# A one-core hybrid block: prefix sums in two halves with the keys' sums beside them, one more unit's convolution on TensorE, and a new planned order

## The chip, the cores and the metric

The kernel runs on one core of one Trainium2 chip. A time is the device time of one execution in microseconds (us). The time before is the median of three runs, 792.27 us (791.22 to 794.27). Engines are named as in the profile: PE is TensorE (PEld its weight loads), DVE is VectorE, ACT is ScalarE, POOL is GpSimd, SP is SyncE, which issues the transfers.

## The reference, cut to what matters

The input x is 8 sequences of 512 tokens with 128 features, all in float32. Four layers follow each other, each as `x = x + layer(layernorm(x))`:

1. Delta rule (attention a): q, k and v are projections followed by a causal convolution over four tokens and SiLU, 16 heads of 8; a state of 8 by 8 per head is updated token by token.
2. Mixture of experts ("f" in the kernel): 8 experts, the best two per token weighed by a softmax; `relu(x W1) W2` with 256 hidden features.
3. Linear attention (attention b): with phi = elu + 1, token i of a head of width 8 gets

```python
A = jnp.einsum('bhid,bhjd->bhij', q, k) * mask
num = jnp.einsum('bhij,bhjd->bhid', A, v) + jnp.einsum('bhid,bhde->bhie', q, S)
den = jnp.sum(A, axis=-1) + jnp.einsum('bhid,bhd->bhi', q, z) + EPS
out = num / den[..., None]
```

4. The same mixture of experts again ("g").

## The kernel before, in words

The 512 tokens are cut into eight units of 64 tokens (c = 0 to 7). A unit holds the 64 tokens of all eight sequences: four tiles of 128 rows (two sequences of 64 tokens each). Every unit goes through the delta rule, then f, linear attention b and g. The delta rule's recurrence (`recurring`) runs over the units one after another, 16 steps of four DVE instructions each per unit, and ties a later unit to an earlier one, as the convolution's border of three tokens and attention b's carried state do. So layers of early units run beside the recurrence of later ones. Unit 7 is split into two halves after the delta rule (`HALVED`).

**Order.** Every piece of work is a generator that yields the engine that it needs next. A `Weaver` runs them against its own table of durations (`duration`, and `weaver.took(...)` for corrections), with priorities per stream (`FAVOURED`, `OFFSETS`; a thousand tuned numbers), and so writes one fixed order of instructions for each engine. On the chip each engine goes through its list in this order and waits on semaphores. Where the plan has PE idle for at least 0.6 us, `keep_busy` emits filler matmuls ("busy", bf16, 512 columns) for seven tenths of the gap (`BUSY`), so that PE's clock is kept up; the number of fillers in a stretch of PE's list tells how much idle time the plan had there.

**Convolution.** `convolved(s)` handles q, k or v of a unit. For units below `TAPS_ON_PE` (0 to 3) the four taps are four accumulating matmuls of 512 columns with weights `wc` (taps times projection, made at the start by `weights_of_taps`). For the other units one matmul projects, ACT copies the result and scales one tap, POOL moves the 3-token border twice, and DVE adds three taps (`scalar_tensor_tensor` on `s_pp_a`). `wc` lies in the buffers of experts 5 to 7 (`resident[5..7]`), so `loading_later_weights` waits for unit 3's projections before it loads these experts.

**Experts.** `moe` normalizes, computes logits, marks the best two experts on DVE (`first_of_largest`), then weighs them (`relative`: a difference, a tanh, two products) and gets `cb`, a weight per token and expert. `all_experts` transposes `cb` on PE (tile `s_pw`), stores it to DRAM, and for each expert loads the row broadcast over 128 partitions (`wt_xsT<-scw`), multiplies it with the transposed tokens on POOL, and runs two first matmuls (`s_ph`) and two second ones (`y_py`), with a ReLU on ACT between (`hT<-s_ph`).

**Linear attention.** `attend` handles one pair of tiles, 16 times in all. The keys' and values' outer products kv (16 heads x 9 x 8 columns, the ninth column a one, which carries the keys' own sums for the denominator) are made on POOL. `by_q` then takes heads 0 to 5, 6 to 10 and 11 to 15 in turn: four matmuls with a 64 x 64 triangle of ones give the prefix sums over 64 tokens (`s_pc<-kv,tri`, 432 or 360 columns, each in a quarter of PE's array), two DVE products with the queries (`qs`) and one DVE reduce (`nd`) follow. The tile kv has one buffer.

Of the kernel before, what the change touches and what calls it, by code (L numbers as in the profile page):

```python
# [10 lines left out]
F32 = mybir.dt.float32  # L11
# [26 lines left out]
TURNED = 1  # L38
# [3 lines left out]
TAPS_ON_PE = 4  # L42
# [4 lines left out]
ADDED_ON_DVE = (4,5,6,7)  # L47
NEAR_NORMS = (5,6,7)
# [5 lines left out]
TURNED_IN = (0,7)  # L54
# [13 lines left out]
PASSES = ()  # L68

FAVOURED = {  # L70
    ("b", 0.0): 1475, ("b", 1.0): -605, ("b", 2.0): 408, ("b", 3.0): -1141, ("b", 4.0): 1159, ("b", 5.0):
    -397, ("b", 6.0): -3095, ("b", 7.0): -2237, ("b", 7.5): -2071, ("beside",): 1509, ("ending",): 696,
    ("f", 0): 1839, ("f", 1): 922, ("f", 2): 673, ("f", 3): -941, ("f", 4): 1648, ("f", 5): 1050, ("f", 6):
    -1587, ("f", 7): 767, ("f", 7.5): -2892, ("g", 0.0): 1576, ("g", 1.0): 901, ("g", 2.0): 357, ("g", 3.0):
    7212, ("g", 4.0): -253, ("g", 5.0): -2424, ("g", 6.0): -246, ("g", 7.0): 1986, ("g", 7.5): -2626,
    ("outputs",): 7, ("prepare", 0): -904, ("prepare", 1): -3306, ("prepare", 2): 224, ("prepare", 3):
    -1571, ("prepare", 4): -839, ("prepare", 5): -16, ("prepare", 6): 680, ("prepare", 7): -2427, ("recur",
    0): 3219, ("recur", 1): -6342, ("recur", 2): -2844, ("recur", 3): 482, ("recur", 4): -2744, ("recur",
    5): -1405, ("recur", 6): 1064, ("recur", 7): -724, ("values",): 149, None: -1498,
# [4 lines left out]
    -5735, -5206, -179, -62, -5753, 0, -6219, -6323, 29, -6838, 1464, 2372, 2338, -2, 1277, -3446, -3136,  # L84
    2417, -3137, -2112, -3119, -3650, -311, 76, 1, 3, -3, 77, -342, -7970, 977, -20, -4091, 3665, -19, 806,
    -4343, -4621, -4648, -4379, 711, 806, -5289, 1734, 1900, 1275, 623, -5269, -420, -380, -832, -1479, 50,
    -758, -790, 125, -3620, 585, -553, 237, 2322, 2064, -5521, 501, -5381, -5928, -3498, -40, 2563, 4086,
    10628, -5495, 782, 11097, 2142, 524, -2998, -175, 1440, -9862, 334, 747, 94, -5047, -6796, 307, 308,
    -1787, -402, -3506, -63, -187, 265, -2927, -6059, -6411, -6618, 0, -4528, -6371, -6553, -6091, -5056,
    263, -538, -1107, -6503, -6983, -6, -6510, -36, -961, -967, 294, 389, -6742, -8230, -142, -7747, -8737,  # L90
    -7250, -7254, -7665, -422, 1935, 282, -996, -6683, -9031, 177, 1221, 466, 360, -7342, 552, -8817, -42,
    -7371, 101, 1699, 247, 245, 186, -7410, 57, 713, -5151, 127, -91, -80, -5933, 56, -6006, -6402, 412,
    -6116, -445, 35, 2434, -4925, -4928, -4874, -938, 1079, 406, -7960, 775, 519, -186, -183, -6551, -7752,
    -7695, -8113, 429, 2079, 1870, 73, 72, 717, 130, -428, -37, 347, 2267, 385, -69, 3340, -640, -367, 165,
    -831, -1483, 0, 486, -5539, -200, -199, -399, -34, 2547, -7582, -106, -2671, 11037, 1388, 1383, 1120,
    -962, 17, -1270, -6162, -175, -5673, 211, 50, -7246, -2444, -7484, -2599, -386, 24, -1456, -1295, -1542,
    449, 95, 3319, -2490, -5181, -17, 250, 1245, 968, 926, -3459, -1, -51, -7241, -6288, -40, -5786, 456, 0,
    2, -7292, 471, -361, -79, -6239, 1121, 209, 228, 171, -490, -335, -1339, -4313, -4533, -173, -162,
    -1885, -4676, -5235, -6460, -342, -6601, -6575, 266, 235, 4646, 4647, 78, -899, -7489, 388, -348, 4,
    2051, 1488, -3366, -170, -1594, -5834, -4738, -590, -6081, 2703, 771, 806, 2101, -1052, -4471, -334,  # L100
    10046, 384, -6869, -6546, 10224, -8058, 323, -1252, 463, 8950, 0, -8361, 1480, -113, -361, -8416, -9767,
    -47, -200, -9523, 27, -8517, -60, 66, -8349, -229, -9575, -9613, 177, 0, -516, 2087, 1808, 1102, -3472,
    -3462, -3444, -261, -48, -604, -199, 8924, -1499, -2626, 0, -5333, -68, 0, -3882, -1964, 1388, 1387,
    -3692, -5022, -5065, -555, 136, 6558, 1420, 1897, 1801, 9994, 299, 277, 324, -41, 8082, 391, 7156, 7157,
    -5841, -322, -1273, -5351, 627, 9366, -2233, -2747, 1391, 674, -7825, -11438, -30, 775, 2023, 1821,
    -1660, -376, -7698, 679, -3112, 1424, -5849, 0, -55, 151, -899, 680, -7529, -8147, 148, 896, 1077, 914,
    339, 108, 425, -1456, -5019, -1472, -477, 2580, -4207, -3854, -4163, -8696, -1145, -4645, -48, -435,
# [360 lines left out]
def duration(key, op, args, kw):  # L468
# [12 lines left out]
    if key == "ACT":  # L481
        table = TABLE_OF.get(args[2]) if op == "activation" else None
        scale = args[2] if op == "mul" else kw.get("scale", 1.0)
        more = (0.19 if "bias" in kw else 0.0) + (0.0 if isinstance(scale, float) else 0.08)
        return key, 0.2 + more + n * 0.76e-3, 0.1, table
    if key == "POOL" and ALU.pow in args:
        return key, 1.05, 0.1
# [1521 lines left out]
```

## Time and profile before

The numbers below are of one profiled execution. The medians in the first row are of other runs.

| quantity | before |
|---|---|
| median of 3 runs | 792.27 us |
| the profiled execution | 790.81 us, of which the span on the core is 789.1 us |
| PE busy (matmuls) | 758.7 us, 96% of the span |
| DVE / ACT / POOL busy | 560.8 / 504.7 / 446.0 us (71 / 64 / 57%) |
| filler matmuls | 195, busy 52.7 us |
| expert matmuls (`s_ph`, `y_py`, f and g) | 530.7 us busy in all |
| granted PE clock, mean | 0.991 |

By stretches of the span, PE idle (the stretch less PE's busy time) and fillers in it:

| stretch, us | PE idle, us | fillers |
|---|---|---|
| 0 to 40 | 5.8 | 61 |
| 40 to 80 | 4.5 | 34 |
| 80 to 120 | 3.5 | 47 |
| 120 to 160 | 1.4 | 10 |
| 160 to 200 | 7.1 | 28 |
| 200 to 240 | 1.7 | 1 |
| 240 to 760 | 1.6 | 4 |
| 760 to 789 | 4.7 | 10 |

A matmul in float32 is two records in this trace, and a record's modelled end overlaps the next one's start. So the time that a matmul takes from the others is read as the distance from its start to the next start, not as its duration. A busy share is an average: PE is the busiest engine, but in the first 240 us it also waits.

### The profile page before, as it was taken

How to read it: one execution, taken by the hardware profiler on the slowest of the kernel's cores; microseconds unless marked ns; L12 is line 12 of the kernel's file. 1: busy time of each engine (PE TensorE's matmuls, PEld its weight loads, DVE VectorE, ACT ScalarE, POOL GpSimd, SP SyncE). 2: the span in 40 equal slices, each digit the busy share in tenths (PEclk: the TensorE clock that was granted, in tenths of full speed). 3: DMA queues.
4: the chain of work that ended last, by engine and by line, in shares of the span. 5: the costliest groups of instructions: out<-in, count | busy, mean ns of one | idle time of the engine just before them, and what ended most of it. 6: DMA issues, size and time to landing. Idle time of an engine off the chain costs nothing.

```text
span 789.1 us, 11578 instructions
## 1 busy us (share of the span) xinstructions
PE 758.7 (96%) x3383; PEld 384.7 (49%) x3383; DVE 560.8 (71%) x1429; ACT 504.7 (64%) x1388; POOL 446.0 (57%) x609
## 2 busy tenths in 40 slices
PE   8888899997999999999999999999999999999997
PEld 4344454553435434544444435453444456644475
DVE  1689898978997698899999799798557145342310
ACT  5765767688877865678676875773664445643352
POOL 1244447659586495775586664877736606735331
PEclk9999899998999999999999999999999999999999
DMA  1451426105233311214132132232112211321121
GB/s 46 118 133 42 123 63 183 45 23 148 69 97 80 98 56 55 81 55 126 54 111 96 34 102 78 82 106 67 42 41 81 60 28 48 108 69 44 37 60 34
DMA packets 82392, 59.67 MB, mean 76 GB/s; under 512 B 48152, under 2 KB 64152, under 8 KB 82328
## 3 DMA queue, kind: packets, MB, share of 16 engines
q1 hardware_dynamic: 81608, 58.64, 25.8%
q8 instruction: 27, 0.44, 0.2%
q10 hardware_dynamic: 720, 0.28, 0.2%
q14 instruction: 37, 0.30, 0.1%
HBM read 46.52 MB, written 12.39 MB: 75 GB/s over the span
## 4 chain that ended last, share of the span: by engine, by line
PE 78%; DVE 11%; ACT 6%; issue 2%; DMA 2%; POOL 1%; SPq 0%; DVEq 0%; ACTq 0%; POOLq 0%
PE s_ph_f L454 14%; PE y_py_f L454 13%; PE s_ph_g L454 13%; PE y_py_g L454 12%; PE s_pc_b L454 5%; PE s_pp_a L454 4%; PE s_pp_b L454 2%; PE busy L1950 2%; PE s_pu_b L454 2%; DVE st L454 2%; PE s_pS_b L454 2%; DVE W L454 1%; ACT squares L454 1%; DVE pj L454 1%; DVE terms L454 1%
## 5 line engine op out<-in xcount | busy, mean ns | idle before, releaser
L454 ACT ACTIVATE hT_g<-s_ph_g 128x512 f32<-128x512 f32 (+1 forms) x144 | 79.0, 552 | 95.5 <-PE s_ph_g L454 94.5
L454 PE MATMUL y_py_f<-hT_f,resident 128*128 128x512 f32 (+1 forms) x288 | 134.3, 555 | 0.3 <-ACT hT_f L454 0.2
L454 PE MATMUL s_ph_f<-wt_xsT_f,resident 128*128 128x512 f32 (+1 forms) x288 | 132.1, 554 | 1.9 <-POOL wt_xsT_f L454 1.1
L454 PE MATMUL y_py_g<-hT_g,resident 128*128 128x512 f32 (+1 forms) x288 | 133.3, 553 | 0.3
L454 PE MATMUL s_ph_g<-wt_xsT_g,resident 128*128 128x512 f32 (+1 forms) x288 | 131.0, 553 | 0.3 <-POOL wt_xsT_g L454 0.2
L454 ACT ACTIVATE hT_f<-s_ph_f 128x512 f32<-128x512 f32 (+1 forms) x144 | 78.7, 550 | 50.9 <-PE s_ph_f L454 49.4
L454 POOL TENSOR_TENSOR wt_xsT_g<-wt_xsT_g,xn_xnT_g 128x512 f32<-128x512 f32 (+1 forms) x69 | 79.0, 1166 | 37.0 <-DMA wt_xsT_g<-scw_g 26.7
L454 POOL TENSOR_TENSOR po<-st,kq 128x256 f32<-128x256 f32 x128 | 93.8, 763 | 3.3 <-DVE st L454 2.7
L454 POOL TENSOR_TENSOR kv_b<-ph_b,v 128x1152 f32<-128x1152 f32 x32 | 69.2, 2176 | 39.8 <-ACT v L454 27.1
L454 POOL TENSOR_TENSOR wt_xsT_f<-wt_xsT_f,xn_xnT_f 128x512 f32<-128x512 f32 (+1 forms) x69 | 79.4, 1168 | 17.5 <-DMA wt_xsT_f<-scw_f 17.4
L454 DVE TENSOR_TENSOR qs_b<-s_pc_b,ph_b 128x360 f32<-128x360 f32 (+1 forms) x96 | 50.4, 551 | 46.2 <-PE s_pc_b L454 45.5
L454 PEld LDWEIGHTS y_py_f<-hT_f,resident 128*128 128x128 f32 x288 | 50.6, 190 | 47.2 <-issue 40.4
L454 PEld LDWEIGHTS s_ph_f<-wt_xsT_f,resident 128*128 128x128 f32 x288 | 50.4, 190 | 47.4 <-issue 31.6
L454 PEld LDWEIGHTS y_py_g<-hT_g,resident 128*128 128x128 f32 x288 | 50.9, 190 | 44.1 <-issue 35.6
L454 PEld LDWEIGHTS s_ph_g<-wt_xsT_g,resident 128*128 128x128 f32 x288 | 50.9, 190 | 43.7 <-issue 32.0
L454 DVE TENSOR_REDUCE st<-terms 128x64 f32<-128x320 f32 x128 | 61.4, 480 | 12.3 <-ACT terms L454 6.0
L454 DVE TENSOR_REDUCE factors<-pj 128x32 f32<-128x288 f32 x128 | 58.4, 456 | 6.2 <-ACT factors L454 2.5
L1950 PE MATMUL busy<-ones 128*128 128x512 bf16 x195 | 52.7, 411 | 9.5 <-ACT o L454 3.4
L454 DVE TENSOR_TENSOR pj<-st,factors 128x256 f32<-128x256 f32 x128 | 53.4, 417 | 4.7 <-ACT factors L454 1.8
L454 DVE TENSOR_TENSOR terms<-factors,kt 128x256 f32<-128x256 f32 x128 | 53.7, 419 | 4.2 <-ACT vn L454 1.1
L454 ACT COPY terms<-st 128x64 f32<-128x64 f32 x128 | 39.6, 309 | 25.0 <-DVE st L454 23.8
L454 POOL TENSOR_TENSOR pq<-y_a,y_a 128x128 f32<-128x128 f32 x32 | 21.1, 685 | 46.2 <-ACT squares L454 23.1
(270 smaller groups left out, 1336.1 us busy)
## 6 DMA issues: line engine op xcount, KB each, us to landing
wt_xsT_f<-scw_f SPq DMA_DIRECT2D x55, 256.0 KB
wt_xsT_g<-scw_g SPq DMA_DIRECT2D x55, 256.0 KB
scr<-y_a SPq DMA_DIRECT2D x24, 256.0 KB
qk<-scr SPq DMA_DIRECT2D x16, 256.0 KB
x_a<-in_x_dram SPq DMA_DIRECT2D x16, 128.0 KB
vv<-scr SPq DMA_DIRECT2D x8, 256.0 KB
sco<-on SPq DMA_DIRECT2D x8, 256.0 KB
oT<-sco SPq DMA_DIRECT2D x8, 256.0 KB
```

The lines of the kernel that those rows point to most:

```text
L454: r = call(*args, **kw)
L1950: nc.tensor.matmul(pt, ones, ones.unsqueeze(1).to_broadcast([P, 4, P]), start=True, stop=True)
```

## The change

The edits, in the order of the diff:

- `TAPS_ON_PE` goes from 4 to 5: unit 4's taps are matmuls too. PE's list gets 12 matmuls of 512 columns with tap weights and loses 3 plain projections; DVE loses 9 `scalar_tensor_tensor`, ACT 3 copies and 3 scalings, POOL 6 border copies. The border that unit 5 needs is now made in unit 5.
- The tap weights lie in the tile kv instead of in experts 5 to 7. Experts 5 to 7 load at once; the first pair's `attend` waits for unit 4's projections before it takes kv.
- kv has eight columns per head instead of nine. `by_q` takes two halves of eight heads: four matmuls of 512 columns, plus two of 128 columns (`s_pk<-keys,tri`) that sum the keys themselves; a new piece `denominators` multiplies these by the queries in PSUM and reduces them. It takes three PSUM banks at once instead of two.
- The weights of the two best experts (`relative`) start as soon as the second maximum is known, beside the marking of the second expert.
- `cb` lies in a 128 x 128 tile that is zero outside the used columns, and the whole tile is transposed.
- The planner's durations for some ACT and POOL operations are changed, a few fixed corrections are added or removed, the plan gets six more passes (`PASSES`), and all priorities (`FAVOURED`, `OFFSETS`) are new. So the order on every engine is new.

Counted in the two programs, PE's list has 1948 matmuls before and 1943 after, of which 195 and 181 are fillers; DVE's list has 1431 and 1438 instructions, ACT's 1263 and 1257, POOL's 614 and 611, SP's 379 and 379. The options `STATES_ON_PE` and `KEYS_ON_POOL` are empty, and `TURNED` names the same four cases as before.

The diff, cut to its core (the tables of priorities and the code of the empty options are left out):

```diff
-TURNED = 1
+TURNED = {"f0": 1, "g0": 1, "f7": 1, "g7": 1}
 QUERIES_ON_POOL = ()
 ELU_ON_POOL = ()
 CORRECTED_ON_POOL = tuple(range(8))
-TAPS_ON_PE = 4
+TAPS_ON_PE = 5
...
+STATES_ON_PE = ()
+KEYS_ON_POOL = ()
+BURST = NE - 3
...
-TURNED_IN = (0,7)
...
-PASSES = ()
+PASSES = ((1, 0.0, {}), (5, 0.1, {}))
...
-        more = (0.19 if "bias" in kw else 0.0) + (0.0 if isinstance(scale, float) else 0.08)
+        more = (0.1 if "bias" in kw else 0.0) + (0.0 if isinstance(scale, float) else 0.06)
         return key, 0.2 + more + n * 0.76e-3, 0.1, table
     if key == "POOL" and ALU.pow in args:
-        return key, 1.05, 0.1
+        return key, 0.4 + n * 0.16, 0.1
     if key == "POOL":
-        return key, 0.2 + n * (1.72e-3 if n > 512 else 2.0e-3), 0.1
+        if op == "tensor_copy":
+            return key, 0.16 + n * 1.3e-3, 0.1
+        return key, 0.18 + n * (1.73e-3 if n > 512 else 2.15e-3), 0.1
...
-    wc = [resident[NE - 3 + s].rearrange("p (k d) -> p k d", k=4) for s in range(3)]
+    kv_ = const.tile([P, 2, NH, HD, HD], F32, name="kv")
+    taps = kv_.rearrange("p w h e d -> p (w h e d)")[:, 0 : 12 * D].rearrange("p (s k d) -> p s k d", s=3, k=4)
+    wc = [taps[:, s] for s in range(3)]
...
+    cbs = [const.tile([P, P], F32, name=f"cb_{i}") for i in range(SETS)]
+    for i in range(SETS):
+        nc.gpsimd.memset(cbs[i], 0.0)
...
-    kvs = held_in(1, [P, 2, NH, V1, HD], "kv")
-    qss = held_in(1, [P, 2, 6 * V1 * HD], "qs")
+    kvs = Slots(weaver, None, None, "kv", 1, [kv_])
+    qss = held_in(1, [P, 2, NH // 2 * HD * HD], "qs")
...
-            if TAPS_ON_PE and e >= NE - 3:
-                yield fired("projected", TAPS_ON_PE - 1, e - (NE - 3))
             for to, by in [(slice(0, NF), f_w1[e])] + [
                 (slice(NF + f * D, NF + (f + 1) * D), f_w2[e, f * P : (f + 1) * P, :]) for f in range(2)
             ]:
                 yield "SP"
                 sp.dma_start(resident[e][:, to], by)
+                if e >= BURST and to.stop < 2 * NF:
+                    weaver.moves(-LANDS)
...
-            pe.transpose(pt[0 : nb * NE, 0:P], cb.rearrange("p b e -> p (b e)"), ident)
+            pe.transpose(pt[:, 0:P], cb_, ident)
...
-            if e < TURNED and int(name[1]) in TURNED_IN:
+            if e < TURNED.get(name[:2], 0):
...
-        m2 = yield from first_of_largest(lg2, 1)
...
+            if k:
+                scales["weights"] = spawn(relative(m1, m))
...
+        yield from first_of_largest(lg2, 1)
+        yield scales["weights"]
+        cb_ = cbs[own]
+        cb = cb_[:, 0 : nb * NE].rearrange("p (b e) -> p b e", b=nb)
...
+        if c == 0:
+            yield from all_of([fired("projected", TAPS_ON_PE - 1, s) for s in range(3)])
         kv = yield from kvs.take(n)
...
-                .to_broadcast([P, NH, V1, HD]),
-                v1[:, w].unsqueeze(3).to_broadcast([P, NH, V1, HD]),
+                .to_broadcast([P, NH, HD, HD]),
+                v1[:, w, :, 0:HD].unsqueeze(3).to_broadcast([P, NH, HD, HD]),
...
-        def by_q(lo, hi):
-            nh = hi - lo
-            m = nh * V1 * HD
-            yield from banks.need(2)
+        def prefixes(to, i, w, src):
+            of = slice(i * CH, (i + 1) * CH)
+            pe.matmul(to[w * CH : (w + 1) * CH], tri[of, of], src[of, w], start=True, stop=True)
+            if i or w:
+                weaver.overlaps(max(1.68e-3 * free_size(to), 0.225) - 0.01)
+
+        def by_q(half):
+            nh = NH // 2
+            lo, m = half * nh, nh * HD * HD
+            yield from banks.need(3)
             pcs = []
             for i in range(2):
-                pc = yield from banks.take(f"pc_{n}_{lo}_{i}")
+                pc = yield from banks.take(f"pc_{n}_{half}_{i}")
                 pcs.append(pc)
+            pk = yield from banks.take(f"pk_{n}_{half}")
             yield "PE"
             for i in range(2):
-                of = slice(i * CH, (i + 1) * CH)
                 for w in range(2):
-                    pe.matmul(
-                        pcs[i][w * CH : (w + 1) * CH, 0:m], tri[of, of],
-                        kvf[of, w, lo * V1 * HD : hi * V1 * HD], start=True, stop=True,
-                    )
-                    if i or w:
-                        weaver.overlaps(1.68e-3 * m - 0.01)
-            qs = yield from qss.take(f"{n}_{lo}")
+                    prefixes(pcs[i], i, w, kvf[:, :, half * m : (half + 1) * m])
+            for w in range(2):
+                prefixes(pk[:, 0:D], half, w, keys)
+            summing = spawn(denominators(half, pk))
+            qs = yield from qss.take(f"{n}_{half}")
             for i in range(2):
                 yield "DVE"
                 dve.tensor_tensor(
-                    qs[:, i, 0:m].rearrange("p (h e d) -> p h e d", h=nh, e=V1),
-                    pcs[i][:, 0:m].rearrange("p (h e d) -> p h e d", h=nh, e=V1),
-                    queries[:, i, lo * HD : hi * HD].rearrange("p (h d) -> p h d", d=HD).unsqueeze(2)
-                    .to_broadcast([P, nh, V1, HD]),
+                    qs[:, i].rearrange("p (h e d) -> p h e d", h=nh, e=HD),
+                    pcs[i].rearrange("p (h e d) -> p h e d", h=nh, e=HD),
+                    queries[:, i, lo * HD : (lo + nh) * HD].rearrange("p (h d) -> p h d", d=HD).unsqueeze(2)
+                    .to_broadcast([P, nh, HD, HD]),
                     ALU.mult,
                 )
                 banks.give(pcs[i])
@@ -1733,10 +1804,18 @@
                     weaver.moves(-DEPENDENT)
             yield "DVE"
             dve.tensor_reduce(
-                nd[:, :, lo:hi].rearrange("p i h e -> p i (h e)"),
-                qs[:, :, 0:m].rearrange("p i (m d) -> p i m d", d=HD), AX.X, ALU.add,
+                nd[:, :, lo : lo + nh, 0:HD], qs.rearrange("p i (h e d) -> p i h e d", h=nh, e=HD), AX.X, ALU.add
             )
             qss.give(qs)
+            yield summing
+
+        def denominators(i, pk):
+            sums = pk[:, 0:D]
+            yield "DVE"
+            dve.tensor_tensor(sums, sums, queries[:, i], ALU.mult)
+            yield "DVE"
+            dve.tensor_reduce(nd[:, i, :, HD], sums.rearrange("p (h d) -> p h d", d=HD), AX.X, ALU.add)
+            banks.give(pk)
 
...
-        summed = [spawn(by_q(lo, hi)) for lo, hi in ((0, 6), (6, 11), (11, 16))]
+        summed = [spawn(by_q(half)) for half in range(2)]
...
-            weaver.took("POOL", 0.8)
```

## The prediction

> **What bounds the kernel now.** I read the page first: the span, the busy shares and the chain that ended last.
>
> ```profile
> span 789.1 us, 11578 instructions
> PE 758.7 (96%) x3383; PEld 384.7 (49%) x3383; DVE 560.8 (71%) x1429; ACT 504.7 (64%) x1388; POOL 446.0 (57%) x609
> PE   8888899997999999999999999999999999999997
> PE 78%; DVE 11%; ACT 6%; issue 2%; DMA 2%; POOL 1%; SPq 0%; DVEq 0%; ACTq 0%; POOLq 0%
> ```
>
> PE is the bound, and its row of tenths says where it isn't: only in the first third and the last slice does a digit fall below 9. Next I read the busy time by stretches of 40 us (the first number after the stretch's length is PE's).
>
> ```profile
> 160.00:200.00 40.00, 32.89 (x185) 18.26 (x184) 31.88 (x78) 34.25 (x100) 29.84 (x47) 0.91 0.32 92
> 240.00:280.00 40.00, 39.69 (x152) 19.89 (x151) 28.55 (x71) 32.10 (x80) 21.76 (x28) 1.00 0.37 99
> 560.00:600.00 40.00, 40.00 (x192) 18.30 (x190) 21.93 (x52) 23.74 (x58) 20.48 (x18) 1.00 0.27 80
> 760.00:789.00 29.00, 24.32 (x110) 18.18 (x108) 1.12 (x4) 9.99 (x27) 7.54 (x11) 0.99 0.18 42
> ```
>
> From 240 to 760 us PE never rests, while DVE falls from 38 us of 40 to 14. So in this part a microsecond of PE work is a microsecond of span, and relief for DVE, ACT or POOL is worth nothing. Before 240 us PE idles 24.0 us and runs 181 of the 195 fillers; there the recurrence and the first units' chains, not PE, set the pace. The span is thus PE's real work, plus fillers, plus idle, and I cost the change in these three terms.
>
> To price PE's work I read its timeline inside the dense part, taking distances from start to start (columns: start, duration, what).
>
> ```profile
> 311.03 1.12 PE L454 MATMUL y_py_g<-hT_g,resident 128*128 128x512 f32 x2
> 312.09 1.44 PE L454 MATMUL s_pc_b<-kv_b,tri 64*64 64x360 f32 x16
> 313.46 1.13 PE L454 MATMUL y_py_g<-hT_g,resident 128*128 128x512 f32 x2
> 314.42 0.38 PE L454 MATMUL s_pt_q_b<-ident,ph_b 128*128 128x128 f32 x2
> 314.73 0.95 PE L454 MATMUL s_pc_b<-kv_b,tri 64*64 64x432 f32 x8
> 315.62 0.66 PE L454 MATMUL s_pty_g<-ident,m_yT_g 128*128 128x128 f32 x4
> 321.38 0.71 PE L454 MATMUL s_pS_b<-sbd,qT_b 128*64 128x144 f32 x8
> 322.02 1.13 PE L454 MATMUL y_py_f<-hT_f,resident 128*128 128x512 f32 x2
> 326.00 1.02 PE L454 MATMUL s_ph_f<-wt_xsT_f,resident 128*128 128x512 f32 x2
> 326.86 1.02 PE L454 MATMUL y_py_f<-hT_f,resident 128*128 128x512 f32 x2
> ```
>
> A 512-column matmul takes 0.86 us (326.00 to 326.86). Two 360-column groups of four take 1.37 and one of 432 takes 0.89. With a fixed part s and k per column, s + 720 k = 1.37 and s + 432 k = 0.89, so k is 1.67 ns and s 0.17 us. The matmul at 311.03 follows one split visit and precedes another and takes 1.06 instead of 0.86: each visit to the split array costs its neighbours 0.20.
>
> **The change, part by part.** The base is the profiled execution, 790.8 us; the median of the runs shown is 1.5 above it.
>
> *Unit 4's taps.* PE gets 12 matmuls and loses 3: 9 x 0.86 = +7.7 us. The others lose work:
>
> ```profile
> L454 DVE SCALAR_TENSOR_TENSOR s_pp_a<-cv_a,cw,s_pp_a 128x512 f32<-128x512 f32 x36 | 26.8, 749 | 5.0 <-ACT s_pp_a L454 4.8
> L454 ACT ACTIVATE s_pp_a<-s_pp_a,cw 128x512 f32<-128x512 f32 x12 | 8.1, 676 | 0.0
> L454 POOL TENSOR_TENSOR kv_b<-ph_b,v 128x1152 f32<-128x1152 f32 x32 | 69.2, 2176 | 39.8 <-ACT v L454 27.1 <-DVE ph_b L454 7.3 <-PE s_ph_f L454 3.2
> ```
>
> DVE loses 9 x 0.749 = 6.7 us, ACT 3 x (0.676 + 0.596 for the copy) = 3.8, POOL 6 x 0.21 = 1.3. In the trace unit 4's taps stand at 172 to 184 us, inside the stretch with PE's largest idle time (7.1 us). PE's waits there:
>
> ```profile
> PE busy L1950 <- ACT v L454: 2.3, 1, 2.3
> PE busy L1950 <- ACT y_a L454: 1.7, 1, 1.7
> PE busy L1950 <- ACT o L454: 1.5, 1, 1.5
> PE busy L1950 <- ACT cT_f L454: 1.3, 1, 1.3
> ```
>
> Only the second, for the SiLU of a unit 4 projection, hangs on these taps. I take -1.7, between 0 (v, at 2.3, is late next) and -7.1 (all idle time of the stretch).
>
> *Prefix sums on PE.* Before: 16 groups at 0.89, 32 at 0.77 (0.17 + 360 x 1.67 ns), and 46 visits in PE's order at 0.20, less 0.3 for two joined pairs: 47.8 us. After: 32 groups at 0.17 + 512 x 1.67 ns = 1.02, 32 visits at 0.20, and 32 pairs `s_pk`. No row shows such a pair. The nearest is `s_pS`, two pairs of 144 columns in 0.64: (0.64 - 0.17) / 2 = 0.235, so 0.21 at 128. Bounds: 0 if a pair runs wholly beside the group, 0.42 if its two don't overlap. Taken at 0.21: 32.6 + 6.4 + 6.7 = 45.7, so -2.1 (bounds -8.8 and +4.6).
>
> *Prefix sums elsewhere.* POOL's 32 products shrink by a ninth: 32 x 0.24 = -7.7 us. DVE's products and reduces took 95.9 us (rows of `qs` and `nd`: 32.1 + 18.3 + 28.7 + 16.8). After: 64 products at 0.69 (a 512-column PSUM add, `ph`), 32 reduces of 1024 at 1.21 (row `o<-po`), and 64 small ones near 0.29 (between 0.19 for 32 elements and 0.42 for 256): 101.4, +5.5. With the taps DVE stands at -1.2. I cost all of this at nothing: 14 of 16 attends lie where PE is dense. Without that cover it would be +5.5.
>
> *The kv tile holds the taps.* The first attend waits for unit 4's projections; behind it on POOL stand the recurrence's output products. In the new order of PE these projections come before f0's first expert, and the first triangle matmul after 54 of the first 64 expert matmuls. So at 0.86 each some 46 us cover the wait: 0. Without the cover, the 10.3 us of projections are its price. Experts 5 to 7 load earlier: nine issues (768 KB) now stand in SP's queue ahead of unit 3's stores, and no longer between units 3 and 4. No PE wait in the trace names such a load, the 16 DMA engines are busy 35% of 80 to 120 us, and the recurrence of unit 2, which ends at 164 us, covers unit 3's transfers: 0. Uncovered it would be one transfer of that queue, 4.3 us (`scr` at 118.64 in the chain).
>
> *Routing.* `relative`, five short operations (those on DVE 0.16 to 0.2 each), no longer follows the marking, about 1 us per routing, 18 routings. But its product now may wait on DVE for POOL's deviation, with the recurrence queued behind it. Only f0 and f1 lie before the dense part: bounds -2 and +2, taken 0. The 18 wider transposes of `cb` cost nothing, 128 moving columns as before. [...]
>
> *The order.* 181 fillers instead of 195, at 0.22 each (20 take 4.5): -3.0. A filler run covers seven tenths of a planned gap, so the plan has another 3/7 of that less idle time: -1.3. The bounds of idle time are those of the rivals. Where the fillers stand differs: up to f0's first expert 162 instead of 144, from there to f1's last 9 instead of 36, after f2's first 6 instead of 14. Up to f1's last expert both orders hold 442 real matmuls.
>
> **Sum:** +7.7 - 1.7 - 2.1 - 3.0 - 1.3 = -0.4: 790.4 as profiled, 792 as a median. The extra PE work and the shorter waits cancel. I forecast no change; half a percent, 4 us, is about what a measurement of this kernel can tell from none.
>
> **The rivals.**
>
> *A, faster: the hole after f0 closes and none opens.* In the trace f0's experts end near 160 us, f1's start at 191.5; 28 fillers and 7.1 us of idle time lie between. In the new order f1 follows f0 with two fillers between. If the idle time of 160 to 240 us (8.8) goes, 7.1 more than I count is gained: 785. For it: DVE and ACT work of unit 4 goes. Against: the 162 fillers up to f0 say that the wait stands earlier now.
>
> *B, slower: the hole moves ahead of f0 and grows.* 29 fillers stand between unit 3's last projection and unit 4's first, and f0's first expert comes 39 real matmuls later. The old hole had 7.1 us of idle time to 28 x 0.22 = 6.2 of fillers; 29 fillers at this rate bring 7.4 beside what is counted, and with unit 4's projections (10.3) waiting too, up to 12: 799 to 804. It decides from 4 us of added idle time before 240 us. Against: DVE reaches f0's routing after only a little more work than before.
>
> *C, slower: the key sums don't overlap.* Each `s_pk` pair takes 0.42 or drains the group before it: +6.7, 799. For it: they go to the row group that a 512-column matmul still uses. Against: `s_pS` pairs do overlap.
>
> **How the numbers follow.** Forecast 0.36, with its own range 787 to 797; A 0.34 (778 to 788); B 0.20; C 0.10. The bounds of the prefix sums (-8.8, +4.6) and of idle time reach from 779 to 804, which leaves out about 0.1 at each end. Faster by over 0.5% (below 788.3): A 0.32, forecast 0.06, so 0.38. Within: forecast 0.25, the edges of the others 0.06, 0.31. Slower: B and C 0.27, forecast 0.04, 0.31.
>
> **What would show it.** In the profile after: PE dense from about 250 to 760; a `s_pc` group with its `s_pk` pair 1.23 apart from the next matmul plus 0.20 around it; nine fewer DVE adds on `s_pp_a`; PE's idle time before 240 us near 21 and no wait of POOL's first `kv` on PE's projections. I am wrong if PE rests in the dense part, if the hole before f0 is larger than the old one, or if that pair costs 0.4.

## The result and the profile after

| | before | after |
|---|---|---|
| median of 7 runs each on one chip | 791.22 us | 799.14 us (797.57 to 799.79) |
| ratio, 95% interval | 1 | 1.0091 [1.0072, 1.0109] |
| span of the profiled execution | 789.1 us | 796.9 us |
| filler matmuls in PE's list | 195 | 181 |

The changed kernel is 0.9% slower, 7.2 us by the ratio (the medians differ by 7.9). The forecast was no change (792).

The page of the changed kernel: span, busy time, PE's tenths in 40 slices, and the chain that ended last.

```profile
span 796.9 us, 11602 instructions
PE 765.4 (96%) x3387; PEld 393.1 (49%) x3387; DVE 557.2 (70%) x1436; ACT 498.8 (63%) x1382; POOL 438.1 (55%) x606
PE   8899898999988999999999999999999999999997
PE 75%; ACT 6%; POOL 5%; DVE 4%; DMA 4%; issue 3%; SPq 1%; POOLq 0%; ACTq 0%; DVEq 0%
```

Two digits of 8 stand at slices 12 and 13, 219 to 259 us, where the kernel before had 9s. DVE's part of the chain fell from 11% to 4% and yet the span grew: other engines stand in its place. The same stretches as before (the stretch, its length, busy time of PE, PEld, DVE, ACT and POOL, then the granted clock, the DMA share and GB/s):

```profile
160.00:200.00 40.00, 39.59 (x170) 19.68 (x168) 33.42 (x83) 30.68 (x85) 26.08 (x45) 1.00 0.32 83
200.00:240.00 40.00, 36.13 (x187) 17.09 (x188) 35.54 (x86) 32.13 (x86) 23.95 (x27) 1.00 0.15 43
240.00:280.00 40.00, 36.34 (x151) 19.42 (x152) 35.59 (x86) 21.49 (x65) 30.26 (x34) 0.91 0.27 85
560.00:600.00 40.00, 39.96 (x154) 19.24 (x154) 22.52 (x54) 24.36 (x62) 26.27 (x34) 1.00 0.26 76
760.00:797.00 37.00, 32.38 (x149) 25.04 (x147) 4.53 (x20) 15.31 (x44) 9.40 (x15) 0.97 0.19 51
```

The old hole after f0's experts is closed: PE is busy 39.59 of 40 us at 160 to 200, where it had 32.89. But from 200 to 280 it rests 7.5 us, where it rested 2.0 (38.33 and 39.69 busy). The row of 200 to 240 in the kernel before:

```profile
200.00:240.00 40.00, 38.33 (x178) 15.76 (x177) 36.71 (x87) 29.53 (x76) 28.46 (x40) 1.00 0.28 80
```

This rest is called the hole below. It is not the whole loss: PE's idle time over the span (the span less PE's busy time) grew only from 30.4 to 31.5 us. Before 240 us it fell from 24.0 to 20.9, behind 240 us it grew from 6.4 to 10.6. The rest of the longer span is PE's busy time, 758.7 before and 765.4 after. PE's timeline of the changed kernel shows what it waits for there (start, duration, what; in brackets the idle time ahead and who ended it):

```profile
234.13 0.66 PE L458 MATMUL s_pt_b<-ident,x_a 128*128 128x128 f32 x4 [0.62 <-DVE x_a L458]
235.46 0.43 PE L458 MATMUL s_pm_b<-xn_xnT_b,wg 128*32 128x128 f32 x8 [0.67 <-ACT xn_xnT_b L458]
238.51 1.27 PE L458 MATMUL s_pc_b<-kv,tri 64*64 64x512 f32 x8 [0.56 <-DVE qs_b L458]
241.46 1.66 PE L458 MATMUL s_pp_b<-wb,xn_xnT_b 128*64 128x128 f32 x10 [1.15 <-DVE qs_b L458]
246.11 0.44 PE L458 MATMUL s_pt_t_b<-ident,xn_att_b 128*128 128x128 f32 x2 [1.29 <-DVE xn_att_b L458]
247.78 1.41 PE L458 MATMUL s_po_b<-wob,xn_xnT_b 128*128 128x128 f32 x8 [1.23 <-ACT xn_xnT_b L458]
250.38 1.22 PE L458 MATMUL s_ph_f<-wt_xsT_f,resident 128*128 128x512 f32 x1
```

f1's experts have ended at 232 us, f2's begin at 250.4, and in PE's list the end of b0, unit 0's linear attention, stands between them. DVE is busy 35.5 of 40 us in each of the two stretches.

The parts that the prediction priced on PE are seen in the dense stretch (the same timeline):

```profile
339.89 1.09 PE L458 MATMUL s_pc_b<-kv,tri 64*64 64x512 f32 x8
340.80 0.39 PE L458 MATMUL s_pk_b<-ph_b,tri 64*64 64x128 f32 x4
341.11 1.12 PE L458 MATMUL y_py_f<-hT_f,resident 128*128 128x512 f32 x2
```

A group takes 0.91 us from start to start and its pair 0.31: 1.22 together, where the prediction has 1.02 + 0.21 = 1.23. And DVE's adds of the convolution went from 36 to 27, as they should:

```profile
L458 DVE SCALAR_TENSOR_TENSOR s_pp_a<-cv_a,cw,s_pp_a 128x512 f32<-128x512 f32 x27 | 19.7, 750 | 0.8 <-ACT s_pp_a L458 0.7
```

### The profile page after: what moved, and what is told of

Same layout as the page of the kernel before. It is cut to its first block, busy times and chain, and to the rows that moved or that the text cites. A ratio compares the mean times of both kernels' runs of the same rounds, so it can differ in the third digit from the quotient of the medians.

```text
span 796.9 us, 11602 instructions
## 1 busy us (share of the span) xinstructions
PE 765.4 (96%) x3387; PEld 393.1 (49%) x3387; DVE 557.2 (70%) x1436; ACT 498.8 (63%) x1382; POOL 438.1 (55%) x606
## 4 chain that ended last, share of the span: by engine, by line
PE 75%; ACT 6%; POOL 5%; DVE 4%; DMA 4%; issue 3%; SPq 1%; POOLq 0%; ACTq 0%; DVEq 0%
PE s_ph_g L458 13%; PE y_py_g L458 13%; PE y_py_f L458 12%; PE s_ph_f L458 12%; PE s_pp_a L458 5%; PE s_pc_b L458 3%; POOL po L458 3%; PE s_pp_b L458 2%; PE s_po L458 2%; ACT squares L458 2%; PE s_pu_b L458 2%; PE s_pS_b L458 1%; DMA qk<-scr 1%; SPq L458 1%; PE s_po_b L458 1%
## 5 line engine op out<-in xcount | busy, mean ns | idle before, releaser
L458 POOL TENSOR_TENSOR kv<-ph_b,v 128x1024 f32<-128x1024 f32 x32 | 62.4, 1964 | 50.2 <-ACT v L458 20.4
L458 PEld LDWEIGHTS s_ph_f<-wt_xsT_f,resident 128*128 128x128 f32 x288 | 51.7, 191 | 45.6 <-issue 35.5
L458 PEld LDWEIGHTS s_ph_g<-wt_xsT_g,resident 128*128 128x128 f32 x288 | 50.2, 190 | 35.5 <-issue 28.0
L458 DVE TENSOR_TENSOR qs_b<-s_pc_b,ph_b 128x512 f32<-128x512 f32 x64 | 42.5, 683 | 18.7 <-PE s_pc_b L458 18.4
L458 PE MATMUL s_pp_a<-xnT_a,kv 128*128 128x512 f32 x120 | 54.1, 596 | 0.4 <-ACT xnT_a L458 0.4
L458 POOL COPY st<-st 128x64 f32<-128x64 f32 x31 | 7.5, 241 | 77.2 <-DVE st L458 77.2
```

Of the source, the lines that this page charges most:

```text
L458: r = call(*args, **kw)
```

## The experiments

Four theories. **Theory 1:** PE's work is the span, so 7.7 us of taps are paid as 7.7. **Theory 2:** the loss is the new hole, which the new order makes by letting f2 come late. **Theory 3:** PE's halved clock behind the waits of the hole (0.50 granted from 242 to 245 us and from 249 to 251) costs the time. **Theory 4:** the order is fitted to its work: chains of several engines arrive together, so that added work is paid and work taken away gives nothing.

In the kernels named x and u, and in r3 against r2, the planner is told the durations of the unedited kernel, so that its order stays; what differs is only what is issued. By the intervals, the difference of two such runs is known to about 2 us. Differences in us are differences of the ratios to the kernel before, times 791.2.

### Work taken from and added to the changed kernel

x1 leaves out nine tap matmuls, x2 issues them twice.

```diff
                 for k in range(4):
                     yield "PE"
+                    if c == 4 and k:
+                        weaver.took("PE", free_size(xnT[:, :, k : k + CH]) * 1.68e-3, 0.2)
+                        continue
```

> The changed kernel with nine of unit 4's twelve tap matmuls left out (the taps 1 to 3 of q, k and v, 512 columns each, 9 x 0.86 = 7.7 us of PE); the planned order of everything else is kept. Theory 1, PE's work is the span: the +7.7 us of my sum is paid in full, the time falls by about 7 from the changed kernel's 799 to 792, level with the kernel before. Theory 2, the order: ahead of f0 PE waits for others anyway, the matmuls are only replaced by waits, and the loss comes from the new hole between f1's and f2's experts (225 to 250 us): 797 to 799, no more than 2 us gained.

> The changed kernel with the same nine tap matmuls issued twice in place (7.7 us more PE work, unit 4's projections come out with three taps doubled). Theory 1: +7.7, 807. Theory 2: waits ahead of f0 swallow a part; 800 to 804. If leaving them out gains nothing while doubling them costs 7 or more, the order is fitted to the work: what is added is paid, what is taken away is not given back.

Measured: x1 799.3, ratio 1.0095 [1.0073, 1.0118]: nothing gained (+0.3). x2 806.8, 1.0188 [1.0164, 1.0213]: +7.7, the full 9 x 0.86. The timeline of x1 shows where 7.7 us went:

```profile
131.45 2.74 PE L458 MATMUL s_pp_a<-xnT_a,kv 128*128 128x512 f32 x6
138.19 0.43 PE L458 MATMUL s_pb_a<-xnT_a,wbeta 128*32 128x128 f32 x8 [4.00 <-ACT y_a L458]
138.55 0.66 PE L458 MATMUL s_pt_f<-ident,m_xs_f 128*128 128x128 f32 x4
142.59 2.07 PE L458 MATMUL s_ph_f<-wt_xsT_f,resident 128*128 128x512 f32 x2 [3.38 <-ACT wt_xsT_f L458]
```

and the changed kernel at the same place:

```profile
131.33 10.47 PE L458 MATMUL s_pp_a<-xnT_a,kv 128*128 128x512 f32 x24
143.42 1.12 PE L458 MATMUL s_ph_f<-wt_xsT_f,resident 128*128 128x512 f32 x2 [0.68 <-ACT wt_xsT_f L458]
```

Unit 4's taps fill the time in which f0's first expert waits for its tokens. Without them PE waits 4.00 and 3.38 us there instead. f0 begins 0.8 us earlier (142.59 instead of 143.42), and by f1's first transpose (`s_pt_f`, 154.10 and 154.18) nothing is left of that. So a microsecond of PE work taken away here is not a microsecond of span; what is left of theory 1 is the direction upwards.

x3 lets fillers be issued where no general PSUM bank (a buffer for the results of matmuls) is free, into a free long bank, one of those that hold the experts' sums.

```diff
+        if gap >= 0.6 and not banks.free and long_banks.free:
+            keep_busy_long(gap)
         if gap < 0.6 or not banks.free or weaver.clock.get("PE", 0.0) < WA_LANDS:
             return
```

> The changed kernel with fillers also where all five general PSUM banks are held: 22 more filler matmuls of 0.22 us, 15 of them in the new hole between 240 and 250 us, written to a free long bank; the order of the rest is kept. Theory 3, the clock: the waits of the hole halve PE's clock on the real work behind them (granted clock 0.71 to 0.78 from 240 to 253 us); with the fillers it stays at 1, and the time falls by 2 to 3.5 us, to about 796. If the clock has no share in the loss: 798.5 to 800, the fillers fill waits and gain nothing. Theory 1 and theory 2 say nothing of it.

Measured: 798.5, 1.0083 [1.0063, 1.0104]: -0.6, not to be told from nothing. From 240 to 250 us the clock did come up. The changed kernel from 240 to 260 us (the clock is the third number from the end):

```profile
240.00:250.00 10.00, 6.33 (x38) 4.93 (x40) 9.40 (x19) 4.05 (x12) 7.54 (x11) 0.76 0.60 185
250.00:260.00 10.00, 10.00 (x44) 5.47 (x43) 8.62 (x22) 5.12 (x16) 9.09 (x9) 0.90 0.08 30
```

and x3:

```profile
240.00:250.00 10.00, 7.21 (x52) 4.07 (x51) 9.94 (x20) 5.82 (x20) 5.92 (x10) 0.99 0.40 127
250.00:260.00 10.00, 10.00 (x38) 5.62 (x38) 9.35 (x21) 3.77 (x10) 9.08 (x8) 0.84 0.23 87
```

So a fast clock from 240 to 250 us gains nothing by itself: there PE works on what DVE and ACT make late. And the slow stretch is not gone, it has moved behind 250 us (0.84 instead of 0.90, and 0.67 from 250 to 255, where it was 0.81), onto f2's first experts. So x3 gives theory 3 no support and does not refute it. x3 shows one thing more. The plan had gaps of at least 0.6 us in the hole, and the kernel issued no filler in them, since all five banks were held. So few fillers are no sign of a full PE.

x4 issues each keys' pair twice, x5 none, x6 leaves out DVE's nine adds of unit 5, which stand ahead of the hole.

```diff
             for w in range(2):
+                nc.tensor.matmul(pk[w * CH : (w + 1) * CH, 0:D], tri[of, of], keys[of, w], start=True, stop=True)
```

> The changed kernel with each of the 32 pairs of 128 columns that sum the keys (s_pk) issued twice, the same result. By the trace of the changed kernel a group of four with its pair takes 1.23 us, the pair 0.315 of it. Theory 1 (each microsecond of PE is one of span): 32 x 0.31 = +10, 809. If a pair really ran beside its group (the lower bound of the prediction, 0): no more than +2. If the pair's two matmuls do not overlap (rival C, 0.42 each): +13, 812.

> The changed kernel with the 32 pairs of matmuls that sum the keys left out (the denominators are made of the queries alone, without the keys' sums; every DVE instruction stays). Theory 1, PE's work is the span where it is dense: 30 of the 32 pairs lie behind 240 us, so -6 (at the 0.20 each that doubling them cost) to -10 (at 0.315 each), 789 to 793. Theory 4, the order is fitted to its work and only added work shows: 0 to -3, 796 to 799.

> The changed kernel with the nine tap adds of unit 5 on DVE left out (6 us of DVE, which stand at 172 to 192 us; unit 5's convolution keeps one tap). In the new order they come before the routing of f2, and f2's late experts leave the hole at 225 to 250 us. If DVE's load ahead of the hole is what makes it (theory 2 with DVE as the bound): -3 to -6, 793 to 796. If the engines' chains arrive there together (theory 4), relief for one of them gives 0 to -1, 798 to 799.

Measured: x4 805.5, 1.0170 [1.0147, 1.0193], +6.3, which is 0.20 a pair on average. x5 799.9, 1.0101 [1.0075, 1.0126], +0.8. x6 798.8, 1.0090 [1.0070, 1.0110], -0.1. Added work costs, and work taken away makes no run shorter, on PE ahead of f0, on PE in the dense stretch and on DVE ahead of the hole. So theory 4 agrees with all five.

For x5 the trace says more than the total. In the profiled execution, which is 1.6 us above x5's median, f2 begins 5.8 us later than the changed kernel's (250.38):

```profile
256.21 1.68 PE L458 MATMUL s_ph_f<-wt_xsT_f,resident 128*128 128x512 f32 x2
```

Its span is only 2.9 us longer (799.8 and 796.9). So behind f2's first expert x5 is 2.9 us quicker, and its total is a gain in the dense stretch against a larger loss in front, at a granted clock of 0.57 from 240 to 260 us. Why the front became later was not asked.

x6 shows that the adds on DVE ahead of the hole do not make it: PE still rests 8.4 us from 200 to 280 us. DVE's load inside the hole (9.40 of 10 us busy from 240 to 250) was taken away in no run, so theory 2 stays open in that form.

### The parts alone, in the old order

These start from the kernel before and keep its order. u1 has unit 4's taps on PE, u2 the halves and the keys' pairs, u3 both. In u2 and u3 the keys' pairs stand in a group of their own, where the last third stood, so PE runs 48 groups in its split array, as before; the changed kernel joins each pair to a half and runs 32. The earlier start of the routing's weights, the wider transposes of `cb` and the earlier loads of experts 5 to 7 are in none of the three.

```diff
+                if c == 4:
+                    for k in range(4):
+                        nc.tensor.matmul(
+                            pp, wc[s][k], xnT[:, :, k : k + CH], start=(k == 0), stop=(k == 3)
+                        )
+                    planned(pe, "matmul", pp, None, xnT[:, :, 3:])
+                else:
                     pe.matmul(pp, wa[:, s * D : (s + 1) * D], xnT[:, :, 3:], start=True, stop=True)
...
-                    pe.matmul(
-                        pcs[i][w * CH : (w + 1) * CH, 0:m], tri[of, of],
-                        kvf[of, w, lo * V1 * HD : hi * V1 * HD], start=True, stop=True,
-                    )
+                    if third < 2:
+                        nc.tensor.matmul(
+                            pcs[i][w * CH : (w + 1) * CH, 0:mm], tri[of, of],
+                            kvf[of, w, third * mm : (third + 1) * mm], start=True, stop=True,
+                        )
+                    else:
+                        nc.tensor.matmul(
+                            pcs[i][w * CH : (w + 1) * CH, 0:D], tri[of, of], keys[of, w], start=True, stop=True,
+                        )
+                    planned(pe, "matmul", Shape([CH, m]), None, Shape([CH, m]))
```

> The kernel before, its planned order kept on every engine, with one part of the change alone: unit 4's taps as 12 matmuls on PE in the place of its 3 projections (9 x 0.86 = 7.7 us more), and its copies, scalings, border moves and nine adds gone from ACT, POOL and DVE. The tap weights lie in memory that is free until then. Theory 1 (PE's work is the span): the prediction's own terms for this part, +7.7 - 1.7 = +6, 797. Theory 2, the part is free where PE waits anyway: the old hole from 160 to 200 us has 10.8 us of idle time, so 0 to +2, 791 to 793. Theory 4, the order is fitted to its work (the chains of all engines arrive together, so added work is paid wherever it is put): +4 to +7, 795 to 798, although the taps in the new order were worth nothing when left out.

> The kernel before, its planned order kept, with the other part alone: kv without the ninth column, heads in two halves of 512 columns in the place of the first two thirds, and in the place of the last third the two pairs of 128 columns that sum the keys, their two products on DVE and one reduce. Per pair of tiles PE does two groups of 0.92 and two pairs of at most 0.32 instead of 0.89 + 2 x 0.77, with as many visits as before; DVE does 4 x 0.68 + 2 x 0.29 + 2 x 1.21 + 0.42 = 6.1 us instead of about 6.0 (rows of qs and nd, 95.9 us over 16). Theory 1: 16 x (2 x 0.92 + 2 x 0.32 - 2.43) = +0.8, 792. The prediction's figure for this part is -2.1, 789, with fewer visits than here. Theory 4: larger pieces arrive later at the same place in the order, +2 to +6, 793 to 797.

> The kernel before, its planned order kept, with both parts (taps of unit 4 on PE, and halves with the keys' pairs in the place of the thirds). It tells what the work of the change costs without the new order: by theory 1 the sum +6.8, 798; by theory 4 +6 to +12, 797 to 803, and then the new order, at 799, is not the cause of the loss but wins some of it back. If it is at 791 to 794, the loss of the changed kernel is the new order's alone.

| kernel | median, us | ratio to before, 95% interval | us over before |
|---|---|---|---|
| u1, taps | 794.98 | 1.0043 [1.0029, 1.0056] | +3.4 |
| u2, halves | 795.01 | 1.0053 [1.0040, 1.0065] | +4.2 |
| u3, both | 798.41 | 1.0099 [1.0085, 1.0113] | +7.8 |
| the changed kernel | 799.14 | 1.0091 [1.0072, 1.0109] | +7.2 |

The two parts add up, and together they are as large as the whole loss. So the new order is not needed for it. The new order with all that u3 leaves out makes -0.6 against u3, inside the intervals; that these are each near nothing, and do not cancel, is not shown.

In u1 PE's waits ahead of f1's and f2's experts (waits of PE from 160 to 260 us: total, times, longest):

```profile
PE busy L1974 <- ACT v L454: 2.2, 1, 2.2
PE s_ph_f L454 <- POOL wt_xsT_f L454: 0.9, 1, 0.9
PE busy L1974 <- ACT cT_f L454: 0.8, 1, 0.8
PE busy L1974 <- ACT o L454: 0.4, 1, 0.4
```

The wait for `y_a` (1.7 before) is gone, those for `o` and `cT_f` shrank by 1.1 and 0.5, a new one of 0.9 came: 2.4 us less. The granted clock of 160 to 200 us is 1.00 instead of 0.91. That the clock gave the rest of the 4.3 us between 7.7 and 3.4 is argued, not shown.

u2 has no more DVE time than the kernel before, but cut otherwise. The groups of DVE before (busy time, mean ns of one, idle time ahead):

```profile
L454 DVE TENSOR_TENSOR qs_b<-s_pc_b,ph_b 128x360 f32<-128x360 f32 x64 | 32.1, 525 | 25.9 <-PE s_pc_b L454 25.3
L454 DVE TENSOR_REDUCE nd_b<-qs_b 128x90 f32<-128x720 f32 x32 | 28.7, 898 | 0.3
L454 DVE TENSOR_TENSOR qs_b<-s_pc_b,ph_b 128x432 f32<-128x432 f32 x32 | 18.3, 602 | 20.3 <-PE s_pc_b L454 20.1
L454 DVE TENSOR_REDUCE nd_b<-qs_b 128x108 f32<-128x864 f32 x16 | 16.8, 1047 | 0.1
```

and in u2:

```profile
L1737 DVE TENSOR_TENSOR qs_b<-s_pc_b,ph_b 128x512 f32<-128x512 f32 x64 | 42.2, 685 | 39.4 <-PE s_pc_b L1722 39.0
L1752 DVE TENSOR_REDUCE nd_b<-qs_b 128x128 f32<-128x1024 f32 x32 | 38.9, 1215 | 0.3
L1745 DVE TENSOR_TENSOR qs_b<-s_pc_b,ph_b 128x128 f32<-128x128 f32 x32 | 8.2, 284 | 8.5 <-PE s_pc_b L1727 8.1
L1757 DVE TENSOR_REDUCE nd_b<-qs_b 128x32 f32<-128x256 f32 x16 | 6.7, 417 | 0.1
```

Both sum to 96 us (95.9 and 96.0). The changed kernel itself has 99.4 there, since it reduces the keys' sums in more pieces. Two runs ask where and on which engine the 4.2 us arise. u4 has the halves in b0's two pairs of tiles alone, u6 is u4 with DVE's pieces of b0 in the sizes of the kernel before, but for four products of 128 columns, which save 1.0 us (0.28 instead of 0.53 each).

```diff
-        summed = [spawn(by_q(lo, hi)) for lo, hi in ((0, 6), (6, 11), (11, 16))]
+        summed = [spawn((by_halves if c == 0 else by_q)(lo, hi)) for lo, hi in ((0, 6), (6, 11), (11, 16))]
```

> The kernel before, its order kept, with halves and key pairs in the place of the thirds for the first unit's two pairs of tiles (b0) alone; the other 14 pairs as before. With all 16 in halves the time was 4.2 us above the kernel before, at the same PE work and the same DVE time. If the loss comes from the front, where PE waits for f2's routing (idle time from 200 to 240 us went from 2.4 to 4.8 us there): +1.5 to +2.5, 792.5 to 793.5. If it is spread evenly over the pairs (each arrives a little later at its place in the order): an eighth of it, +0.5, not to be told from no change.

> The kernel with halves in b0 alone (2.7 us above the kernel before), with the DVE instructions of b0's prefix sums given back the sizes of the kernel before (products of 432 and 360 columns, reduces of 864 and 720 elements; only the keys' two products stay at 128 columns), while PE keeps its groups of 512 and POOL its smaller products. b0's sums are then not those of the reference. If the loss comes from DVE, where the first two pieces take 0.68 and 1.21 in the place of 0.53 to 0.60 and 0.90 to 1.05 and what stands behind them comes later: back to the kernel before, 791 (0 to +1). If it comes from PE's longer groups: still +2 to +3, 793 to 794.

Measured: u4 793.8, 1.0034 [1.0020, 1.0048], +2.7 for two of 16 pairs. u6 791.2, 1.0003 [0.9985, 1.0021], +0.2. PE's waits from 200 to 260 us in the kernel before:

```profile
PE s_pt_b L454 <- DVE x_a L454: 1.4, 1, 1.4
PE s_pt_g L454 <- ACT hT_f L454: 0.3, 1, 0.3
PE busy L1950 <- DVE qs_b L454: 0.2, 1, 0.2
```

in u4:

```profile
PE s_pt_b L454 <- DVE x_a L454: 2.1, 1, 2.1
PE s_pm_b L454 <- ACT xn_xnT_b L454: 0.5, 1, 0.5
PE s_pt_g L454 <- ACT hT_f L454: 0.3, 1, 0.3
PE s_pty_f L454 <- ACT m_yT_f L454: 0.3, 1, 0.3
```

and in u6:

```profile
PE s_pt_b L454 <- DVE x_a L454: 1.2, 1, 1.2
PE s_pm_b L454 <- ACT xn_xnT_b L454: 0.5, 1, 0.5
PE s_pt_g L454 <- ACT hT_f L454: 0.3, 1, 0.3
PE s_pty_f L454 <- ACT m_yT_f L454: 0.3, 1, 0.3
```

By the medians it is DVE. In b0 the first two pieces now hold products of 0.68 instead of 0.53 to 0.60 and a reduce of 1.21 instead of 0.90 to 1.05. What stands behind them in DVE's queue, f1's sum `x_a`, comes later; on it waits `s_pt_b`, and behind that in PE's list stand f2's experts. DVE's timeline in the kernel before, in u4 and in u6:

```profile
235.66 0.68 DVE L454 TENSOR_TENSOR x_a<-x_a,s_pty_f 128x512 f32<-128x512 f32 x1
237.08 0.68 DVE L454 TENSOR_TENSOR x_a<-x_a,s_pty_f 128x512 f32<-128x512 f32 x1
235.71 0.68 DVE L454 TENSOR_TENSOR x_a<-x_a,s_pty_f 128x512 f32<-128x512 f32 x1
```

With the old sizes on DVE and PE's groups still at 512 columns, `x_a` is back in its place and the median is back at that of the kernel before. But these 1.4 us are only half of the 2.7. In u4 f2's first two matmuls then take 3.26 us instead of 1.82, at a granted clock of 0.59 from 240 to 244 us, where the kernel before has 1.00. The profiled execution of u6 has a slow clock there too (3.51 us, 0.80) and is 1.1 us above u6's median. So the delay through DVE's sizes is shown, and how much the slower clock behind the wait adds is not.

Where the other pairs of u2 lose can be read by the starts of the same transposes in the two traces, which have one order. Against the kernel before, u2 is 1.4 us early at 206 us (`s_pt_f`), 1.6 late at 250 (`s_pt_g`), 2.5 late at 331, still 2.5 at 564, and 3.4 at the end of the span. So 3.0 us arise from 206 to 250 us, and from 331 to 564, where PE is dense, the halves cost nothing.

### Is it the work or the order?

r1 and r2 are the changed kernel and the kernel before with other priorities alone, found by the same random search for a shorter planned end. r3 puts u3's edits into the order of r2. p1 to p3 have no tuned priorities; p2 and p3 keep the changed planner, with its durations and its six more passes, and p1 the old one.

```diff
-    favoured = {**FAVOURED, **dict(zip(sorted(weaver.keys), OFFSETS, strict=True))}
+    favoured = {}
```

> The changed kernel with other priorities alone (FAVOURED and OFFSETS after a random search of about 15,000 plans, which shortened its planned end from 803.7 to 798.5 us); every instruction is the same, the order is new. If the loss sits in the order (theories 2 and 4), the chip follows the plan: -3 to -6, 793 to 796. If it is the work (theory 1): 798 to 800.

> The kernel before with other priorities alone, after the same search (12,000 plans, planned end from 800.3 to 795.7 us). It is the control: if the chip follows the plan, -3 to -5, 786 to 788, which beats both kernels, and the distance to the searched new work, 5 to 8 us, is what the change of work costs at equal care for the order. If the priorities of the kernel before were at the chip's own optimum, 791 to 794.

> Both parts of the change (unit 4's taps on PE; halves and the keys' pairs in the place of the thirds) put into the searched order of the kernel before, which alone takes 787.8 us; the order is kept on every engine. In the unsearched old order both parts cost +7.8. If that price is a property of the work, it comes again: +6 to +9, 794 to 797, below the changed kernel (799) and above the kernel before (791). If the price were an accident of one order: 788 to 791.

> The kernel before with no tuned priorities at all (FAVOURED and OFFSETS left out): the planner orders by its chains alone; its planned end goes from 800 to 906 us. The chip ran 5 to 10 us below the plan in the tuned kernels, so 890 to 900. It is the base for the next two runs.

> The changed kernel with no tuned priorities: planned end 868 us, so about 860. If the change's work costs 8 us in any order (theory 1): above the run of the old work without priorities. If what it costs belongs to fitted orders (theory 4): the planner's unfitted order waits in other places, and there the new work is faster by some 30 us (4%), with the sign of the measured result turned.

> The changed kernel with no tuned priorities and with unit 4's taps on DVE again (TAPS_ON_PE = 4): planned end 845 us, so about 838. By theory 1 it is 6 us below the run with five units' taps on PE, by the plan 24 below. Together with the two others it splits the unfitted difference into the taps and the rest.

| kernel | median, us | ratio to before, 95% interval |
|---|---|---|
| r1, new work, searched | 800.48 | 1.0111 [1.0088, 1.0133] |
| r2, old work, searched | 787.80 | 0.9947 [0.9926, 0.9967] |
| r3, new work in r2's order | 793.64 | 1.0034 [1.0022, 1.0046] |
| p1, old work, no priorities | 888.61 | 1.1230 [1.1197, 1.1263] |
| p2, new work, no priorities | 867.73 | 1.0966 [1.0927, 1.1006] |
| p3, new work, four units' taps, no priorities | 850.04 | 1.0743 [1.0711, 1.0774] |

r2 beats both kernels; it is 4.2 us below the kernel before with the same instructions but for the fillers (179 instead of 195). r1 gained nothing, although its plan was 5.2 us shorter: it has the same hole (PE rests 8.2 us from 200 to 280 us, f2's first expert comes at 251.1). r3 repeats the price in a second order: 1.0034 / 0.9947 = 1.0088, +6.9 us. So the price of 0.9% came in both orders that were fitted to the old work, and the two orders fitted to the new work (the changed kernel and r1) are no cheaper. Where no order is fitted the sign turns: p2 is 21 us below p1, and p3, with the taps of unit 4 back on DVE, 18 below p2. So there the taps on PE cost, and the rest of the change wins 39 us. That this is the work's gain is not shown: the planner's durations and passes changed too, and no run has the old work with the new planner. Moreover, p2 and p3 do not compute the reference's values, for a cause that is not known, so I take from them the size of the time and no more.

## Why the prediction was wrong, step by step

*"A microsecond of PE work is a microsecond of span" from 240 to 760 us.* Half right. Added work costs: x4's pairs 0.20 each. Taken away it gave no shorter run (x1 +0.3, x5 +0.8), though x5's trace has 2.9 us of gain behind f2's start, lost again in front. The row of 9s says that PE is seldom idle, not that the others have slack.

*Unit 4's taps, +7.7 - 1.7.* The term 7.7 holds for added taps (x2: +7.7). In the old order the hole took more than the one wait that I counted: u1 gives +3.4 instead of +6.0. In the new order the taps lie in f0's wait (x1).

*Prefix sums on PE, -2.1.* The sum of the rows was right by a trade: group 0.91 instead of 1.02, pair 0.31 instead of 0.21. Rival C's pair of 0.42 is refuted. u2 does not test the -2.1: its pairs stand in groups of their own, and PE's part there is +0.8 by the reckoning put ahead of that run.

*Prefix sums elsewhere, "I cost all of this at nothing: 14 of 16 attends lie where PE is dense".* This is the step that failed. The cover holds from 331 to 564 us, but the two attends outside are enough: +2.7 in b0 alone, gone with DVE's old sizes (u4, u6), and +4.2 for all 16 (u2) where PE's part explains +0.8. I priced DVE by its total. The total did not decide it: with an unchanged total (96 us) the first pieces grew and what queues behind them came late. The prediction named +5.5 as the price without cover (the changed kernel's rows give +3.5); it should have asked which two pairs have none. These runs are in the old order. In the changed kernel's own order no run gave any of the 7.2 us back, so how they arise there stays open.

*Fillers -3.0 and idle time -1.3.* This term failed too: it stood for -4.3, and the new order with what u3 leaves out is worth -0.6 against u3. The 14 fillers went, and before 240 us PE's idle time fell as forecast (24.0 to 20.9, the forecast was near 21). But behind 240 us it grew by 4.2 us, where the prediction had nothing. The reckoning from fillers to planned idle time fails where no bank is free, as x3 shows.

*kv's wait for the taps, the experts' loads, routing: 0.* No wait on any of them shows in the changed kernel's hole. The first product into kv starts at 211.2 us, and unit 4's last tap ends at 141.8, so the cover for kv held. None of the three was isolated in a run. As for the wider transposes of `cb`, `s_pw` takes 0.27 us in both traces, and the 512-column matmul behind one 0.86 to the next start (346.65 to 347.51 before, 359.87 to 360.73 after).

*The rivals.* A's first half came true (the old hole closed), its second did not (one opened). B's price (799 to 804) came true by luck: it asked for 4 us of added idle time before 240 us, and there it fell by 3.1; the new hole lies between f1 and f2. The old order gives the same loss with a rest of only 2.9 us from 200 to 280 (u3), so a hole of this size is not needed for the loss.

The sum of the runs: +3.4 and +4.2, together +7.8 in the old order; -0.6 for the new one and what u3 leaves out; +7.2 measured. Against it stood +6.0, -2.1 and -4.3. So the halves cost 6.3 us more than forecast, the order gave 3.7 less, and the taps cost 2.6 less.

## What to carry to other kernels

In a kernel whose order is fitted by hand or search, price a change by what it adds at each place in each queue, not by totals and not by one engine's busy row: what was taken away made no run shorter in three (x1 +0.3, x5 +0.8, x6 -0.1), what was added was paid in two (x2 +7.7, x4 +6.3). A piece made larger at an unchanged total delays what queues behind it (u4: `x_a` 1.4 us later); look first at the places where the bounding engine waits. And a search over the order gave the old work 0.5% (r2) and the new work nothing (r1), while the change lost 0.9% in fitted orders.

## What was not expected of the hardware

The granted clock fell to 0.76 from 240 to 250 us (0.50 from 242 to 245), where PE was busy 6.3 of 10 us and no single wait of PE is above 1.3 us. With fifteen more fillers (x3), PE busy 7.2 us, the clock there was 0.99, and the slow stretch came later (0.67 from 250 to 255 us); the time moved by 0.6 us, within the noise. That several short waits bring the clock down is my estimate from these two runs, in which the fillers moved the slow stretch and did not end it.

A pair of 128 columns beside a group in the 64 x 64 array takes 0.31 us by the timeline, but a second pair behind it, x4, added 0.20 us each to the run, on average. Why it adds less was not asked.
